# Two 7x7 involutions and a residual convolution block: the next strip's transposes issued between a stage's last tap product and its first column product

## The chip, the cores and the metric

The kernel runs on one core of a Trainium2 chip. Time is the device time of one execution in microseconds (us). Before the change it is 1824.14 us, the median of 8 executions between 1815.97 and 1828.26. The profile shown here is of one of these executions, which took 1827.25 us.

The core's engines work side by side, each through its own list of instructions in order: TensorE (PE: matrix products, whose weight loads have a row of their own, PEld), VectorE (DVE), ScalarE (ACT), GpSimd (POOL) and SyncE (SP, which here only issues transfers). POOL also issues transfers. PE writes its products to PSUM; the other engines copy them from there to SBUF.

## The reference

The input is x, 4 images of 256 channels by 56 x 56, in float32. Four layers follow one another, each as x = x + f(group norm of x) with 32 groups:

- layer 0, an involution: per pixel, a 64-long vector h is made from the 256 channels, and from h a 7 x 7 kernel for each of 16 groups of 16 channels; the output is the sum over the 49 taps of kernel times shifted input;
- layer 1, two 3 x 3 convolutions with batch norms and a residual;
- layer 2, an involution with batch norms and relus;
- layer 3, a spatial and channel gate built on Fourier sums.

```python
h = einsum('bchw,oc->bohw', x, reduce_w) + reduce_b
kern = einsum('bchw,oc->bohw', h, span_w) + span_b      # 7*7 taps x 16 groups
out = (kern * patches).sum(axis=3)                      # patches: the 49 shifted copies of x
```

The change is in the function that does both involutions, layers 0 and 2.

## The kernel before

An involution layer works through 8 stages, one for each image `b` and each half `cb` of its channels (128 channels, 8 groups), so there are 16 stages in the program: 8 in layer 0, in the first 525 us, and 8 in layer 2, from 1250 us on. The convolutions of layer 1 lie between them. `in_order` fixes every engine's instructions in the order in which the code emits them, so nothing is reordered by a scheduler.

A stage has two parts.

**Taps** (`tap_matrices`, line 560). 32 groups of 6 tap products turn h into the matrix `kt`, which holds for each window of 9 x 14 input pixels and each output pixel in it the weight of that input pixel. A group's products go to one PSUM buffer, and are copied to `kt` with the bias added: by ACT for every third group (line 582, six instructions; groups 0, 3, ... 30), by DVE for the others (line 589; group 31 is the last).

**Columns** (`apply`, line 601). The image is cut into 7 columns of 8 pixels, and each column into 19 windows of 3 rows. For a column, PE multiplies the transposed input windows `xw` by `kt` (line 613): first part A, 20 products, then part B, 36 products, each part in a PSUM buffer of its own. ACT takes the first slice of each part (line 626 in layer 0, 628 in layer 2), DVE adds the others (line 633), and the result is added into the image: in layer 0 by POOL (line 638), in layer 2 by DVE (line 640). The very first product of A needs tap groups 0 to 15 alone; the second needs groups up to 31.

**Strips and windows.** The input of a column is first normalised into a strip of 128 channels by 14 pixel columns (`next_strip`): in layer 0 by POOL (line 381), in layer 2 by ACT (line 379). There is one strip tile, so a new strip is written only after the old one has been transposed. `next_windows` then transposes the strip with 7 PE transposes (line 398) into a PSUM buffer, copies it to `xw` with ACT (line 399), and shifts two further copies of it within `xw` by four transfers (lines 405 and 407; SP issues them, but in layer 0 POOL issues the last). `xw` has three tiles, and the windows made in column k of a stage serve column k+3.

In a column the code emits: the products and additions of `apply`, then `next_windows` (transposes, copy, transfers), then `next_strip`, then sums and whatever else is laid into that place. So on PE a column's products are followed by the transposes of a strip that was written during the column before's end; on POOL in layer 0 the order is two additions (638), the transfer (407), the strip (381); on ACT in layer 2 it is the first slices of A and B (628), the copy (399), the strip (379).

**PSUM buffers.** `two_banks` hands out four buffers in turn to whoever asks. A new user waits until the user four requests earlier has been read. In the steady columns the turn is A, B, transposes, A, B, transposes, and so on.

Layer 2 also carries gate work of the image before: POOL loads pieces of it, computes (lines 780 to 787) and stores them, in the stages of images 1 to 3.

Of the kernel before, what the change touches and what calls it, by code (L numbers as in the profile page):

```python
# [16 lines left out]
P = 128  # L17
# [18 lines left out]
Q = QY * QX  # L36
# [3 lines left out]
NSB = 7  # L40
# [31 lines left out]
def net_kernel(  # L72
# [19 lines left out]
    nc = tc.nc  # L92
# [34 lines left out]
    ident_sb = const.tile([P, P], F32, name="ident_sb")  # L127
# [152 lines left out]
    def involution_layer(layer, xin, xout, red, span, sb, xs_of, ahead=None, pending=None):  # L280

        with ExitStack() as es:
# [5 lines left out]
            def two_banks():  # L288

                return banks.tile([P, 2, 512], F32, name="ps")  # L290
# [66 lines left out]
            strips, xws = [], []  # L357
# [25 lines left out]
            def window(ty):  # L383

                k, j = divmod(ty, TY)
                return (0, NSB, 2 * NSB - 1)[j] + k

            def next_windows():

                if len(xws) == len(columns):  # L390
                    return
                flat = strips[len(xws)].rearrange("p h w -> p (h w)")
                xw = work.tile([Q, NTY, P], F32, name="xw", bufs=NXW)
                xws.append(xw)

                ps = two_banks().rearrange("p i n -> p (i n)")
                for k in range(NSB):
                    nc.tensor.transpose(ps[:Q, k * P : (k + 1) * P], flat[:, k * Q : (k + 1) * Q], ident_sb)  # L398
                nc.scalar.copy(xw[:, :NSB, :], ps[:Q, : NSB * P].rearrange("q (n c) -> q n c", n=NSB))  # L399

                n = NSB - 1
                for j in range(1, TY):
                    cut = TY * QX * j
                    at = window(j)
                    nc.sync.dma_start(xw[: Q - cut, at : at + n, :], xw[cut:Q, 0:n, :])  # L405
                    eng = nc.sync if layer == 2 or j == 1 else nc.gpsimd
                    eng.dma_start(xw[Q - cut : Q, at : at + n, :], xw[:cut, 1 : 1 + n, :])
# [152 lines left out]
            def tap_matrices(b, cb, hooks):  # L560

                hp = h_of[b]
                kt = big.tile([Q, GB, TP // PB, NT, PB], F32, name="kt")
                for n in range(GB // 2 * TP // PB):
                    gp, pb = divmod(n, TP // PB)
                    ps = two_banks()
                    for k in range(PB):
                        py, px = divmod(pb * PB + k, TX)
                        z0 = ZF - py * QX - px
                        for i in range(2):  # L570
                            nc.tensor.matmul(  # L571
                                ps[:Q, i, k * NT : (k + 1) * NT],
                                z_sb[i * R : (i + 1) * R, cb * GB // 2 + gp, z0 : z0 + Q],
                                hp[i * R : (i + 1) * R, py, px].rearrange("p a t -> p (a t)"),
                                start=True,
                                stop=True,
                            )
                    g0, p0 = 2 * gp, pb * PB
                    if n % 3 == 0:
                        for i in range(2):  # L580
                            for k in range(PB):
                                nc.scalar.activation(  # L582
                                    kt[:, g0 + i, pb, :, k],
                                    ps[:Q, i, k * NT : (k + 1) * NT],
                                    AF.Identity,
                                    bias=zb_sb[:, cb * GB + g0 + i, p0 + k : p0 + k + 1],
                                )
                    else:
                        nc.vector.tensor_tensor(  # L589
                            kt[:, g0 : g0 + 2, pb],  # L590
                            ps[:Q, :, : PB * NT].rearrange("q i (k t) -> q i t k", k=PB),
                            zb_sb[:, cb * GB + g0 : cb * GB + g0 + 2, p0 : p0 + PB]
                            .unsqueeze(2)
                            .to_broadcast([Q, 2, NT, PB]),
                            ALU.add,
                        )
                    for h in hooks.get(n, ()):
                        h()
                return kt
# [348 lines left out]
            for i in range(NXW):  # L948
                hooks0.setdefault(2 + 5 * i, []).extend((next_windows, next_strip))
# [34 lines left out]
            for u, (b, cb) in enumerate(units):  # L984
# [21 lines left out]
                if b + 1 < B:  # L1006
                    n = 16 if layer == 0 else (26, 21)[cb]
# [8 lines left out]
                elif last_image:  # L1016
                    place(hooks, g2, (1,))
                    hooks.setdefault(16, []).append(ahead[0])
                kt = tap_matrices(b, cb, hooks)

                early = [[] for _ in range(NTX)]
                late = [[] for _ in range(NTX)]
# [46 lines left out]
                for tx in range(NTX):  # L1069
                    if layer == 2 and u == len(units) - 1 and tx == NTX - 1:  # L1070
                        column_sums(tx - 1)
                    for f in early[tx]:
                        f()
                    apply(b, cb, kt, tx, xws[u * NTX + tx])
                    next_windows()
                    next_strip()
                    if tx > 0 and not (layer == 2 and u == len(units) - 1 and tx == NTX - 1):
                        column_sums(tx - 1)
                    for f in late[tx]:
                        f()  # L1080
# [553 lines left out]

    ahead = [begin_conv] + [lambda part=part: begin_weights(part) for part in range(3)]
    st = involution_layer(0, src[0], src[1], red0, span0, sb0, {}, ahead)
    blocks = {}

# [4 lines left out]

    pending = conv_layer(src[1], src[2], st, begin_last)
    involution_layer(2, src[2], src[3], red2, span2, sb2, blocks, pending=pending)


# [63 lines left out]
```

## Time and profile before

| | us |
|---|---|
| median of 8 executions | 1824.14 |
| the profiled execution | 1827.25 |
| its span, from first to last instruction | 1825.1 |
| PE busy | 1725.1 |
| DVE busy | 1375.7 |
| ACT busy | 846.2 |
| POOL busy | 429.3 |
| PE busy in 0 to 525 us, layer 0 | 490.88 |
| PE busy in 525 to 1250 us, layer 1 | 715.04 |
| PE busy in 1250 to 1825 us, layer 2 and the gate | 519.15 |

Several views are used. The page's groups list, for each line and engine, the number of instructions, their busy time and the engine's idle time just before them, with what ended it. The timeline lists an engine's instructions in order of time, neighbours of one line merged: start, length, what, and in brackets the idle time before it and what ended that. The view of waits adds up such idle times. The chain of waits follows the work that ended last back from releaser to releaser.

### The profile page before, as it was taken

What the parts mean: (1) busy time and instruction counts of PE and PEld (TensorE: products, weight loads), DVE (VectorE), ACT (ScalarE), POOL (GpSimd) and SP (SyncE); (2) the same over time, 40 slices, a digit from 0 to 9 for tenths busy, and PEclk for the clock granted to TensorE, in tenths of its full rate; (3) what the DMA queues carried; (4) which work ended last, traced back from release to release, by engine and by line L of the source; (5) the groups of instructions that cost most, each with busy time, mean ns of one, the idle gap of its engine ahead of it and who ended that gap; (6) DMA issues with size and microseconds to landing.
All of it is one profiled execution on the core that took longest, in us unless ns stands there. A gap on an engine that the chain in (4) does not pass through costs nothing.

```text
span 1825.1 us, 55841 instructions
## 1 busy us (share of the span) xinstructions
PE 1725.1 (95%) x24034; PEld 1518.1 (83%) x24034; DVE 1375.7 (75%) x2729; ACT 846.2 (46%) x1981; POOL 429.3 (24%) x626
## 2 busy tenths in 40 slices
PE   7999999999899999999999999997999899899898
PEld 6898889888878988998899889985977787787786
DVE  3787777776689988898889988874777587677675
ACT  3666556555542312322222212104767567567564
POOL 2333432245210000000000000000000564563672
PEclk9999999999989999999999999998999899999996
DMA  2545534454641201111111111132534666765653
GB/s 85 157 151 165 164 116 147 152 157 131 196 161 54 69 26 62 63 69 38 62 60 59 59 42 33 38 129 68 165 129 132 180 207 182 207 207 157 188 151 109
DMA packets 66003, 215.75 MB, mean 118 GB/s; under 512 B 13237, under 2 KB 20926, under 8 KB 62046
## 3 DMA queue, kind: packets, MB, share of 16 engines
q1 hardware_dynamic: 48718, 145.24, 25.3%
q0 software_dynamic: 14688, 64.78, 11.1%
q8 instruction: 189, 3.10, 0.7%
q10 hardware_dynamic: 2352, 2.18, 0.4%
q14 instruction: 56, 0.46, 0.1%
HBM read 76.30 MB, written 49.15 MB: 69 GB/s over the span
## 4 chain that ended last, share of the span: by engine, by line
PE 77%; DVE 8%; ACT 6%; DMA 5%; issue 2%; SPq 1%; POOL 0%; ACTq 0%; DVEq 0%; POOLq 0%
PE mm L1482 19%; PE ps L571 17%; PE ps L613 16%; PE mm L1400 10%; PE mm L1371 5%; PE ps L398 4%; DMA xw<-xw 4%; ACT kt L582 4%; PE ps L450 1%; DVE kt L589 1%; ACT xw L399 1%; DVE un L633 1%; PE ps L696 1%; ACT hp L469 1%; SPq L405 1%
## 5 line engine op out<-in xcount | busy, mean ns | idle before, releaser
L613 PE MATMUL ps<-kt,xw 126*32 126x48 f32 (+1 forms) x12544 | 383.5, 236 | 41.6 <-DMA xw<-xw 15.2
L613 PEld LDWEIGHTS ps<-kt,xw 126*32 126x32 f32 (+1 forms) x12544 | 344.4, 123 | 86.9 <-issue 46.1
L571 PE MATMUL ps<-hp,z_sb 64*126 64x133 f32 x6144 | 391.9, 281 | 15.2 <-ACT kt L582 7.5
L571 PEld LDWEIGHTS ps<-hp,z_sb 64*126 64x126 f32 x6144 | 368.9, 187 | 33.4 <-ACT kt L582 13.5
L1482 PE MATMUL mm<-v,u_sb 128*128 128x280 f32 (+1 forms) x1728 | 385.0, 384 | 3.4 <-DVE v L1307 3.4
L589 DVE TENSOR_TENSOR kt<-ps,zb_sb 126x798 f32<-126x798 f32 x336 | 319.7, 981 | 89.3 <-PE ps L571 88.8
L1482 PEld LDWEIGHTS mm<-v,u_sb 128*128 128x128 f32 x1728 | 327.5, 190 | 57.9 <-DVE v L1307 3.8
L582 ACT ACTIVATE kt<-ps,zb_sb 126x133 f32<-126x133 f32 x1056 | 307.5, 443 | 94.2 <-PE ps L571 93.5
L1400 PE MATMUL mm<-v,u_sb 128*128 128x252 f32 (+1 forms) x936 | 212.0, 387 | 2.6 <-DVE v L1291 2.6
L1400 PEld LDWEIGHTS mm<-v,u_sb 128*128 128x128 f32 x936 | 177.7, 191 | 33.3 <-issue 2.7
L1519 POOL DMA_DIRECT2D x<-xs x24 | 13.1, 547 | 682.7 <-DVE xs L1518 427.4
L633 DVE SCALAR_TENSOR_TENSOR un<-ps,s,un 128x240 f32<-128x240 f32 x224 | 102.4, 457 | 94.4 <-ACT un L628 90.3
L633 DVE SCALAR_TENSOR_TENSOR un<-ps,par_sb,un 128x240 f32<-128x240 f32 x224 | 97.9, 456 | 91.0 <-ACT un L626 86.7
L1467 ACT ACTIVATE res<-xs,shift,norm_sb 128x1120 f32<-128x1120 f32 (+1 forms) x24 | 30.2, 1259 | 235.1 <-DVE xs L1518 107.2
L399 ACT COPY xw<-ps 126x896 f32<-126x896 f32 x112 | 101.7, 908 | 48.1 <-PE ps L398 39.5
L638 POOL TENSOR_TENSOR xs<-un,xs 128x240 f32<-128x240 f32 x112 | 72.3, 666 | 199.6 <-DVE un L633 199.6
L398 PE MATMUL ps<-ident_sb,strip_sb 128*126 128x128 f32 x784 | 111.0, 282 | 0.7 <-DVE un L633 0.7
L626 ACT ACTIVATE un<-ps,par_sb 128x240 f32<-128x240 f32 x112 | 50.3, 449 | 120.7 <-PE ps L613 119.4
L628 ACT ACTIVATE un<-ps,bn_t,s 128x240 f32<-128x240 f32 x112 | 60.2, 539 | 89.4 <-PE ps L613 85.0
L1371 PE MATMUL mm<-xs,u_sb 128*128 128x126 f32 (+1 forms) x792 | 98.5, 277 | 1.2 <-DVE xs L1334 0.9
L139 POOL TENSOR_TENSOR norm_sb<-norm_sb,mhalf 128x1 f32<-128x1 f32 x32 | 19.8, 620 | 334.5 <-DVE norm_sb L138 334.4
L1371 PEld LDWEIGHTS mm<-xs,u_sb 128*128 128x128 f32 x792 | 94.4, 191 | 2.4 <-issue 1.0
(254 smaller groups left out, 1996.5 us busy)
## 6 DMA issues: line engine op xcount, KB each, us to landing
xw<-xw SPq DMA_DIRECT2D x168, 252.0 KB
xw<-xw SPq DMA_DIRECT2D x224, 126.0 KB
xw<-xw POOLq DMA_DIRECT2D x56, 252.0 KB, 4.6
xs<-x SPq DMA_DIRECT2D x24, 560.0 KB
x<-xs POOLq DMA_DIRECT2D x8, 1568.0 KB, 8.4
xs<-x SPq DMA_DIRECT2D x8, 1568.0 KB
xs<-in_x_dram SPq DMA_DIRECT2D x6, 1568.0 KB
x<-xs SPq DMA_DIRECT2D x6, 1568.0 KB
```

Of the source, the lines that this page charges most:

```text
L398: nc.tensor.transpose(ps[:Q, k * P : (k + 1) * P], flat[:, k * Q : (k + 1) * Q], ident_sb)
L399: nc.scalar.copy(xw[:, :NSB, :], ps[:Q, : NSB * P].rearrange("q (n c) -> q n c", n=NSB))
L571: nc.tensor.matmul(ps[:Q, i, k * NT : (k + 1) * NT], z_sb[i * R : (i + 1) * R, cb * GB // 2 + gp, z0 : z0 + Q], hp[i * R : (i + 1) * R, py ...
L582: nc.scalar.activation(kt[:, g0 + i, pb, :, k], ps[:Q, i, k * NT : (k + 1) * NT], AF.Identity, bias=zb_sb[:, cb * GB + g0 + i, p0 + k : p0 ...
L589: nc.vector.tensor_tensor(kt[:, g0 : g0 + 2, pb], ps[:Q, :, : PB * NT].rearrange("q i (k t) -> q i t k", k=PB), zb_sb[:, cb * GB + g0 : cb ...
L613: nc.tensor.matmul(v[m * j : m * j + m, i, :, k * TP : (k + 1) * TP], xw[:, window(ty), m * j : m * j + m], kt[:, ng * j : ng * j + ng, :, ...
L628: nc.scalar.activation(part, o[0], AF.Identity, bias=bn["t4"][:, cb : cb + 1], scale=bn["s4"][ng][:, 0, cb : cb + 1])
L633: nc.vector.scalar_tensor_tensor(part, o[e], s, part, ALU.mult, ALU.add)
L638: nc.gpsimd.tensor_tensor(dst, u, dst, ALU.add)
L1371: nc.tensor.matmul(ps[:, co * m : (co + 1) * m], u[ci][:, co * P : (co + 1) * P], v2[:, e, : n // 2, ci * WT : (ci + 1) * WT], start=(ci = ...
L1400: nc.tensor.matmul(ps, u1_sb[:, ci, dy, k, co * P : (co + 1) * P], v[:, k, dy * NB + ci : (dy + n - 1) * NB + ci + 1 : NB, :], start=(j == 0),
L1482: nc.tensor.matmul(ps, u2_sb[:, ci, dy, k, co * P : (co + 1) * P], v[:, k, dy * NB + ci : (dy + n - 1) * NB + ci + 1 : NB, :], start=(j == 0),
```

## The change

The 7 transposes and the PSUM buffer that they write are taken out of `next_windows` into `begin_windows`. `next_windows` calls it only where it has not been called already, so columns 1 to 6 of every stage, and the windows made during the first stage's taps, are as before. At the end of each stage's `tap_matrices` the code now calls `begin_windows` once. With that, the transposes that stood behind the last product of column 0 stand ahead of its first one. The ACT copy, the transfers and the next strip stay where they were, behind the additions of column 0. The PSUM buffer is asked for before that of column 0's part A, so the turn of the buffers at the head of a stage is transposes, A, B, A, B, transposes, A, and so on.

```diff
+            begun_windows = []
+
+            def begin_windows():
+
+                flat = strips[len(xws)].rearrange("p h w -> p (h w)")
+                ps = two_banks().rearrange("p i n -> p (i n)")
+                begun_windows.append(ps)
+                for k in range(NSB):
+                    nc.tensor.transpose(ps[:Q, k * P : (k + 1) * P], flat[:, k * Q : (k + 1) * Q], ident_sb)
+
             def next_windows():
 
                 if len(xws) == len(columns):
                     return
-                flat = strips[len(xws)].rearrange("p h w -> p (h w)")
+                if not begun_windows:
+                    begin_windows()
+                ps = begun_windows.pop()
                 xw = work.tile([Q, NTY, P], F32, name="xw", bufs=NXW)
                 xws.append(xw)
 
-                ps = two_banks().rearrange("p i n -> p (i n)")
-                for k in range(NSB):
-                    nc.tensor.transpose(ps[:Q, k * P : (k + 1) * P], flat[:, k * Q : (k + 1) * Q], ident_sb)
                 nc.scalar.copy(xw[:, :NSB, :], ps[:Q, : NSB * P].rearrange("q (n c) -> q n c", n=NSB))
...
                 kt = tap_matrices(b, cb, hooks)
 
+                begin_windows()
+
                 early = [[] for _ in range(NTX)]
```

## The prediction

> **What bounds the kernel now.** The page first. PE is busy nearly throughout, and the chain of waits runs over it.
>
> ```profile
> PE 1725.1 (95%) x24034; PEld 1518.1 (83%) x24034; DVE 1375.7 (75%) x2729; ACT 846.2 (46%) x1981; POOL 429.3 (24%) x626
> ...
> PE 77%; DVE 8%; ACT 6%; DMA 5%; issue 2%; SPq 1%; POOL 0%; ACTq 0%; DVEq 0%; POOLq 0%
> ...
> L398 PE MATMUL ps<-ident_sb,strip_sb 128*126 128x128 f32 x784 | 111.0, 282 | 0.7 <-DVE un L633 0.7
> ```
>
> So only PE's idle time is to be won, and the transposes (line 398) hardly wait for anything today. The view of waits for PE says where products of line 613 do:
>
> ```profile
> PE ps L613 <- DMA xw<-xw: 15.2, 8, 3.4
> PE ps L613 <- ACT kt L582: 11.0, 13, 0.9
> PE ps L613 <- DVE sf L762: 2.5, 3, 0.9
> ```
>
> The last two lines are 16 waits of at most 0.9 us: one per stage. PE's timeline at the third stage of layer 0 shows the place.
>
> ```profile
> 170.63 14.18 PE L571 MATMUL ps<-hp,z_sb 64*126 64x133 f32 x240 [0.17 <-ACT kt L582]
> 184.73 0.41 PE L613 MATMUL ps<-kt,xw 126*64 126x96 f32 x2
> 185.98 3.22 PE L613 MATMUL ps<-kt,xw 126*64 126x96 f32 x110 [0.84 <-ACT kt L582]
> 189.13 0.98 PE L398 MATMUL ps<-ident_sb,strip_sb 128*126 128x128 f32 x7
> 190.05 3.24 PE L613 MATMUL ps<-kt,xw 126*64 126x96 f32 x112
> 193.22 0.98 PE L398 MATMUL ps<-ident_sb,strip_sb 128*126 128x128 f32 x7
> ```
>
> Call the first column product's start E (184.73). The next needs the last `kt`, which comes at E+1.25. In between PE idles 0.84 us. In all 16 stages that second start lies at 1.25 to 1.26.
>
> **What the change moves.** Seven transposes per stage, 189.13 to the next product at 190.05: 0.92 us (0.91 in the chain of waits). Moved to E, they end at E+0.91, and the one early product (two passes) takes 0.12 more: E+1.03, still short of E+1.25. Column 0 then runs as before and ends 0.91 us after where it would have carried transposes, so PE reaches column 1 0.91 us earlier: at most 16 x 0.91 = 14.6 us. Nothing is added, no instruction on DVE, ACT, POOL or SP changes its place.
>
> New waits on PSUM, each costed at nothing. The transposes take the buffer of tap group 28, which DVE has read by 183.77, before E; part A that of 29, read by 184.68. In three stages of layer 2 gate products sit between, and part A takes the buffer of group 30, read by ACT at 1426.62, 0.57 after its E of 1426.05 and before the transposes end. Only part B of column 1 is new: it takes the transposes' buffer, so it waits for the ACT copy, behind column 0's first slice of B. By ACT's rows that slice ends at 189.75 and the copy takes 0.91: 190.66. Column 1 would start at 189.14, and its part A takes 2.1 (from 190.05 to 192.33 when ACT takes it up, less 0.15): part B at 191.2. In layer 2 the same sum leaves 0.5 too. Were this cover gone, everything behind on PE would wait by the excess.
>
> Now what is late next: the transposes of column 1. They need the next strip. In layer 0 POOL makes it, by its timeline in the same stage:
>
> ```profile
> 190.28 1.29 POOL L638 TENSOR_TENSOR xs<-un,xs 128x240 f32<-128x240 f32 x2 [18.02 <-DVE un L633]
> 191.52 0.58 POOL L407 DMA_DIRECT2D xw<-xw  x1
> 192.15 1.00 POOL L381 TENSOR_SCALAR strip_sb<-xs,norm_sb 128x784 f32<-128x784 f32 x1
> ```
>
> POOL runs without a break from column 0's additions to the strip's end at 193.15, and its start hangs on DVE's slices of column 0, which stand at E+1.25 as before. The transposes start at 193.22 today, 0.07 later. PE would now be there at 192.31, and must wait until 193.2. The copy coming earlier (189.75 for 190.20) doesn't help: the transfer of line 407 waits for the additions (191.57), not for the copy (191.11). So in layer 0 the gain is given back one column on, with all of column 2 queued behind the waiting transposes. Strip end to transposes is, over the eight stages, 0.20, 0.07, 0.07, 0.10, 0.10, 0.12, 0.07 and 0.10 us. The handover itself takes between nothing and 0.07, the smallest seen, so layer 0 wins between 0.83 and 0.27 us together. I take 0.3, the handover having a price in every row.
>
> In layer 2 ACT makes the strip, and earlier:
>
> ```profile
> 1432.29 1.05 ACT L379 ACTIVATE strip_sb<-xs,norm_sb 128x784 f32<-128x784 f32 x1
> 1434.58 0.98 PE L398 MATMUL ps<-ident_sb,strip_sb 128*126 128x128 f32 x7
> ```
>
> Strip ready at 1433.34, transposes at 1434.58: 1.24 us to spare, and the copy ahead of it on ACT starts 0.36 earlier. So the 0.91 passes column 1 in all eight stages of layer 2: at most 7.3 us.
>
> There transfers decide. In the two stages before gate work starts no column waits for `xw`: 2 x 0.91 = 1.8. The six others (from 1426) keep the DMA engines 53 to 70% busy (the others of layer 2: 41%), and PE waits in four of them, worst here:
>
> ```profile
> 1447.80 2.51 PE L613 MATMUL ps<-kt,xw 126*64 126x96 f32 x28 [3.44 <-DMA xw<-xw]
> ```
>
> Column 3 needs its windows 0.91 earlier, but their copy, and so SP's four transfers, start only 0.36 to 0.45 earlier; for column 4 both move by 0.91. If the engines have room, a stage keeps its 0.91; if landing times hang on the gate's traffic, which POOL paces by itself, it keeps nothing. More than 0.91 or a loss needs the traffic to fall in another order: the same column waited 2.17 to 3.44 in its three worst stages, so 1.3 either way is the spread that order alone makes. I take the middle of nothing and 0.91, 0.45, as no row is nearer to one end: 6 x 0.45 = 2.7.
>
> Sum: 0.3 + 1.8 + 2.7 = 4.8 us. Against the profiled execution (span 1825.1, with 2.15 around it 1827.25) that is 1822.4; that execution is 3.1 above the median, so on the median 1824.14 - 4.8 = **1819.3**. Bounds of its terms: 0.3 + 1.8 + 0 = 2.1 and 0.8 + 1.8 + 5.5 = 8.1 saved, that is 1816.0 to 1822.0.
>
> **A rule on POOL and DVE.** In the changed kernel column 1's slices on DVE (line 633) lie 0.9 us earlier, over the strip on POOL (192.15 to 193.15) instead of over its last 0.3 us. The trace has a pair that suffers from such an overlap: line 640 on DVE, 0.41 us median, 1.38 at most, beside the gate work on POOL. The Trainium skill, SBUF — State Buffer, section "SBUF: two separate sides", says that the two share a port pair under an exclusive lock, which DVE takes with two SBUF inputs or in a two-port mode. Line 640 has two SBUF inputs, and agrees; line 633 reads one from PSUM, so by that rule the strip keeps its 1.00 us and the sum stays. If any overlap counted, layer 0 would lose instead (third rival). No row of before shows a strip wholly under line 633.
>
> **Rivals.**
> - *The strip is no limit.* POOL's spans are called rough by the page; if the strip is usable well before its recorded end, layer 0 keeps 8 x 0.91 = 7.3 and the whole is 16 x 0.91 = 14.6: 1809.5. For it: the transposes have never been seen to wait, so the true time of the strip is only bounded from above. Against: POOL's order is fixed, and the additions that precede the strip are real.
> - *Transfers take all.* The six loaded stages give back everything: 2.1 saved, 1822.0. For it: the waits of up to 3.44; against: POOL issues its second round of gate transfers at 1438.18, and with the change all four transfers of column 1's windows (1436.53 to 1439.04 today) would go out by then. The Trainium skill, DMA: Bandwidth & Descriptors, section "Issuing engines are not separate DMA queues", has SP's and POOL's transfers interleave on the same 16 engines. By that rule alone this case comes out; the latencies in the loaded stages agree.
> - *POOL's strip is slowed by DVE.* At 0.74 us a stage, what line 640 was once slowed by in the row at 1435.73 (1.15 for 0.41 us), layer 0 loses 8 x 0.74 = 5.9 in place of winning 0.3: 1825.5, no change.
> - *Slower: the shifted windows run into the gate's transfers.* Column 3 has its windows with little to spare in the loaded stages (one waits 0.50 already, at 1638.82), and loses half a microsecond of it; if a transfer falls behind a gate piece, a column waits like the 3.44 above. Two such new waits in each of three stages cost 6 x 2.5 = 15 less 4.8: 1834. It decides from 1.7 us lost per loaded stage (10.3 in all: 4.8 plus 5.5).
>
> **Chances.** 0.3% is 5.5 us, about what a measurement of this kernel can tell from no change: below 1818.7 is faster. Forecast 0.55; no limit by the strip 0.13; transfers take all 0.14; slowed strip 0.08; collisions 0.10. The forecast lies 0.6 us from the bound, so a little under half of it, 0.27, is faster: with the first rival 0.40. Same: 0.28 + 0.14 + 0.08 = 0.50. Slower: 0.10. The range takes in the forecast, the transfers' case, the slowed strip and the nearer part of the first rival: 1811 to 1826; the forecast's own is 1816 to 1822.
>
> **What would show it.** PE's timeline at E: 7 transposes, then the two early passes, then a wait of about 0.2 us in place of 0.84, the second product still at E+1.25. Layer 0: the transposes at the end of column 1 with an idle time of about 0.85 released by POOL's strip, column 2 starting where it did. Layer 2: no wait there, column 1 0.91 us earlier, and in the loaded stages waits for `xw` in columns 3 to 5 larger by about 0.45 a stage. The prediction is wrong if the layer 0 wait is missing, if part B of column 1 waits for the copy, or if the `xw` waits change by more than the gain.

## The result, and the profile after

| | before | after |
|---|---|---|
| median of the runs that were compared, us | 1824.58 (66 runs) | 1816.83 (24 runs) |
| ratio of times, 95% interval | | 0.996 [0.9949, 0.9971] |
| the profiled execution, us | 1827.25 | 1819.61 |
| its span, us | 1825.1 | 1817.8 |

The change saves 0.4%: (1 - 0.996) x 1824.58 = 7.3 us, by the interval 5.3 to 9.3. The forecast was 4.8 us saved and 1819.3 us.

In the changed kernel the transposes are line 396, the column products 622, the tap products 580, the copies to `kt` 591 (ACT) and 598 (DVE), the additions on DVE 642 and on POOL 647, the copy to `xw` 408 and POOL's transfer 416. The strips keep their lines, 381 on POOL and 379 on ACT. These are the page's rows for PE, for the chain of waits, and for the transposes (the last column: idle time just before them, and what ended it).

```profile
PE 1723.3 (95%) x24034; PEld 1515.5 (83%) x24034; DVE 1378.8 (76%) x2729; ACT 843.9 (46%) x1981; POOL 431.1 (24%) x626
...
PE 77%; DVE 8%; ACT 5%; DMA 4%; issue 2%; POOL 2%; SPq 1%; ACTq 0%; POOLq 0%; DVEq 0%
...
L396 PE MATMUL ps<-ident_sb,strip_sb 128*126 128x128 f32 x784 | 110.7, 282 | 5.8 <-POOL strip_sb L381 5.6
```

PE does the same work. POOL has gone from 0 to 2% of the chain, and the transposes, which hardly waited before (0.7 us), now wait 5.6 us for POOL's strip. The view of waits for PE (total, times, longest) says the same, and that the sixteen waits of column products for the last `kt` are gone: no line of 622 names ACT's `kt` or DVE's `sf` any more.

```profile
PE ps L622 <- issue: 15.7, 17, 2.0
PE ps L622 <- DMA xw<-xw: 13.7, 11, 4.9
...
PE ps L396 <- POOL strip_sb L381: 5.6, 8, 0.8
```

The place itself, the third stage of layer 0, on the timelines of PE, POOL and DVE (start, length, what, and in brackets the idle time before it):

```profile
183.48 0.98 PE L396 MATMUL ps<-ident_sb,strip_sb 128*126 128x128 f32 x7
184.39 6.77 PE L622 MATMUL ps<-kt,xw 126*64 126x96 f32 x224
191.94 0.98 PE L396 MATMUL ps<-ident_sb,strip_sb 128*126 128x128 f32 x7 [0.78 <-POOL strip_sb L381]
```

```profile
189.02 1.30 POOL L647 TENSOR_TENSOR xs<-un,xs 128x240 f32<-128x240 f32 x2 [18.02 <-DVE un L642]
190.26 0.58 POOL L416 DMA_DIRECT2D xw<-xw  x1
190.89 1.00 POOL L381 TENSOR_SCALAR strip_sb<-xs,norm_sb 128x784 f32<-128x784 f32 x1
```

```profile
190.70 1.81 DVE L642 SCALAR_TENSOR_TENSOR un<-ps,par_sb,un 128x240 f32<-128x240 f32 x4 [0.88 <-ACT un L635]
```

E is, as in the prediction, the place right behind the last tap product, where the first column product stood before: 184.73 there, 183.47 here. Two columns, 224 products, now follow the transposes with no idle time that this view counts; between the starts of the second early pass and the second product 0.19 us are left, where 1.10 lay before. Then PE stands 0.78 us until the strip that ends at 191.89 (190.89 + 1.00). From E to that strip's end it is 8.42 us, as it was before the change (from 184.73 to 193.15). The length of a stage is taken here and below from the start of its last tap product (0.20 us ahead of E) to the start of its last column product: 29.18 us against 29.19, so nothing is kept.

In layer 2 ACT makes the strip. The same place in its second stage, on PE and on ACT:

```profile
1348.18 0.98 PE L396 MATMUL ps<-ident_sb,strip_sb 128*126 128x128 f32 x7
1349.09 6.76 PE L622 MATMUL ps<-kt,xw 126*64 126x96 f32 x224
1355.78 0.98 PE L396 MATMUL ps<-ident_sb,strip_sb 128*126 128x128 f32 x7
```

```profile
1353.14 0.90 ACT L408 COPY xw<-ps 126x896 f32<-126x896 f32 x1
1353.92 1.05 ACT L379 ACTIVATE strip_sb<-xs,norm_sb 128x784 f32<-128x784 f32 x1
```

The strip ends at 1354.97 (1353.92 + 1.05), 0.81 us ahead of the transposes that read it, and they follow the products without a gap. This stage went from 35.44 to 34.57 us.

With the gate's traffic beside it a stage can still lose all of it. Here, in the stage whose last tap product starts at 1419.82, PE gets as far as the first 8 products of column 4 (counted from 0), and waits for windows:

```profile
1436.67 0.62 PE L622 MATMUL ps<-kt,xw 126*64 126x96 f32 x8
1442.21 4.43 PE L622 MATMUL ps<-kt,xw 126*64 126x96 f32 x104 [4.92 <-DMA xw<-xw]
```

In the same column of the same stage the wait was 3.44 us before, and the stage is 0.3 us longer than it was (35.42 for 35.12).

Two other loaded stages, the second halves of images 1 and 2 in layer 2, lose part of it at the first product of column 2. These are PE, DVE and POOL in the first of the two:

```profile
1493.86 3.26 PE L622 MATMUL ps<-kt,xw 126*64 126x96 f32 x112 [0.65 <-ACT xw L408]
```

```profile
1489.81 0.87 DVE L649 SCALAR_TENSOR_TENSOR xs<-un,xs 128x240 f32<-128x240 f32 x1
...
1491.06 0.88 DVE L649 SCALAR_TENSOR_TENSOR xs<-un,xs 128x208 f32<-128x208 f32 x1
...
1492.25 1.46 DVE L642 SCALAR_TENSOR_TENSOR un<-ps,s,un 128x240 f32<-128x240 f32 x3
```

```profile
1489.26 1.15 POOL L795 TENSOR_TENSOR gn<-gn,sfb 128x448 f32<-128x448 f32 x1
1490.49 1.21 POOL L796 TENSOR_TENSOR gx<-gx,gn 128x448 f32<-128x448 f32 x1
```

Products of line 437, for the next image, stand between the transposes and column 2 there and take a PSUM buffer in the turn, so column 2's part A gets the buffer of column 1's part A. DVE has read it at 1493.71 (1492.25 + 1.46), and the product starts 0.15 us later; in the second of the two stages it starts 0.14 us after DVE's read, and there the profile names DVE. DVE is late because two of its additions of line 649 lie beside POOL's sums for the gate and take 0.87 and 0.88 us. In the changed kernel without gate work (below) the same two take 0.41 and 0.37, and PE doesn't wait. In all six profiled executions that have the move in layer 2 and the whole gate work, both stages have this wait, 0.18 to 0.91 us each; in no execution without the move does either have it.

Stage lengths, added up from PE's timeline, in the two profiled executions:

| us | before | after |
|---|---|---|
| layer 0, stages 1 to 7 | 231.8 | 232.9 |
| layer 0, stage 8 | 34.3 | 30.6 |
| layer 2, the two stages without gate work | 64.77 | 62.99 |
| layer 2, the six with it | 212.4 | 210.9 |

These two executions differ by 7.3 us in span, the same as the change saves by the ratio, but that they agree is chance: half of it, 3.8 us, is stage 8 of layer 0, through waits for windows (4.1 us before, 1.0 after) that scatter from one execution to the next. Other executions with the move in layer 0 and the late strip have 30.8 to 32.8 us for this stage, and others without it 31.3 to 33.3.

### The profile page after: what moved, and what is told of

Its sections match the earlier page's. It is cut to its first block, busy times and chain, and to the rows that moved or that the text cites. A ratio compares the mean times of both kernels' runs of the same rounds, so it can differ in the third digit from the quotient of the medians.

```text
span 1817.8 us, 55835 instructions
## 1 busy us (share of the span) xinstructions
PE 1723.3 (95%) x24034; PEld 1515.5 (83%) x24034; DVE 1378.8 (76%) x2729; ACT 843.9 (46%) x1981; POOL 431.1 (24%) x626
## 4 chain that ended last, share of the span: by engine, by line
PE 77%; DVE 8%; ACT 5%; DMA 4%; issue 2%; POOL 2%; SPq 1%; ACTq 0%; POOLq 0%; DVEq 0%
PE mm L1493 20%; PE ps L580 17%; PE ps L622 14%; PE mm L1411 10%; PE mm L1382 5%; PE ps L396 5%; DMA xw<-xw 4%; ACT kt L591 2%; PE ps L459 2%; DVE un L642 1%; DVE kt L598 1%; ACT xw L408 1%; SPq L414 1%; PE ps L705 1%; PE ps L928 1%
## 5 line engine op out<-in xcount | busy, mean ns | idle before, releaser
L622 PE MATMUL ps<-kt,xw 126*32 126x48 f32 (+1 forms) x12544 | 379.3, 236 | 32.6 <-issue 15.7
L396 PEld LDWEIGHTS ps<-ident_sb,strip_sb 128*126 128x126 f32 x784 | 84.2, 141 | 16.7 <-POOL strip_sb L381 6.8
```

The source lines that it names most:

```text
L622: nc.tensor.matmul(v[m * j : m * j + m, i, :, k * TP : (k + 1) * TP], xw[:, window(ty), m * j : m * j + m], kt[:, ng * j : ng * j + ng, :, ...
```

## The experiments

**The change in one layer at a time.** First the changed kernel once more, beside the two halves of it, to have all three on one chip against the same runs of before.

> The changed kernel itself once more, beside the three kernels that take it apart, for the same chip and a second profile. Both theories: 7 to 8 us (0.996) faster than before, as recorded. If the 2.9 us beyond the forecast 4.8 come from chance in one profile (the last stage of layer 0 is 3.8 us shorter in it), the second profile shows that stage at another length; if the change brings them, at the same.

Measured: 1818.66 us against 1823.36, ratio 0.9965 [0.9949, 0.9981], 6.4 us saved (3.5 to 9.3). The last stage of layer 0 took 31.6 us in this execution against 30.6 in the first profile, and 32.1 in the kernel that moves nothing in layer 0 (below): most of its 3.8 us was chance.

```diff
-                begin_windows()
+                if layer == 0:
+                    begin_windows()
```

> Transposes ahead of column 0 in layer 0 alone. Theory of the strip: each of the 8 stages gives its 0.91 us back at column 1's transposes, 0.3 us in all stays (0 to 0.8): ratio 1.000. Rival, both layers gain alike: half of what the change brings, 3.9 us, 0.998. Rival, the gain beyond the forecast sits at the end of layer 0: about 3 us, 0.998. The profile tells the two apart: eight waits of 0.7 to 0.85 us for POOL's strip at the end of column 1 under the first theory.

Measured: 1824.71 us, ratio 1.0001 [0.9986, 1.0016]. The waits of PE in it:

```profile
PE ps L396 <- POOL strip_sb L381: 6.1, 8, 0.8
```

Eight waits, one per stage of layer 0, of 0.76 us on average, in place of eight of 0.85: what is won at the first product is paid at the strip. That the strip is no limit, that both layers gain alike, or that some 3 us of the gain sit at the end of layer 0, is out by this ratio.

```diff
-                begin_windows()
+                if layer == 2:
+                    begin_windows()
```

> Transposes ahead of column 0 in layer 2 alone. Theory of the strip: all that the change brings, 7 to 7.5 us (7.3 is eight times 0.91), 0.996, with no wait for a strip. Rival, both layers gain alike: 3.9 us, 0.998. Rival, the gain beyond the forecast sits at the end of layer 0: 4.5 us, 0.9975.

Measured: 1819.33 us, ratio 0.998 [0.9964, 0.9996], 3.6 us saved (0.7 to 6.6). In layer 0 (the window from 60 to 500 us) the old waits are back and there is none for the strip:

```profile
PE ps L622 <- ACT kt L591: 6.8, 8, 0.9
```

So the gain is layer 2's, but it is half of the 7 to 7.5 us that were expected of it, which lie outside the interval. The halves add up to 3.4 us, below the 6.4 of both together, but their intervals are 3 us wide to each side, and the two don't contradict each other.

**The strip brought forward.** If the strip is what holds layer 0 back, an earlier strip must give the time back. The transposes have read the strip tile by E+0.91 now, so POOL, idle during the taps, can write the next one at once:

```diff
                 begin_windows()
+                if layer == 0:
+                    next_strip()
...
-                    next_strip()
+                    if layer == 2 or tx > 0:
+                        next_strip()
```

> The changed kernel, with column 0's next strip of layer 0 issued on POOL right behind the early transposes instead of behind column 0's additions (the strip tile is free by then, and POOL idles). Theory of the strip: the eight waits of column 1 for POOL (5.6 us in the profile after) go, and 8 x 0.85 = 6.8 us more stay: 14.5 us faster than before, 0.992, unless column 2's transposes wait next, for which POOL's chain of column 1 also starts 0.9 us earlier. Rival, the strip is only the label of the wait and another of its semaphores (DVE) ends it: as the changed kernel, 0.996.

Measured: 1815.26 us, ratio 0.9952 [0.9936, 0.9968], 8.8 us saved against before. And in a second series of the same kernel:

> The early strip once more, beside the two strips on the same chip. Theory, as its first run: even stages of layer 0 keep 0.85 us, odd ones 0.2 to 0.6, some 4.5 us in all on top of the change: 11 to 12 us less than before, 0.9938; its first run gave 0.9952 (0.9936 to 0.9968). Rival, the strip's relief is lost elsewhere: 7 us, 0.996, as the change alone.

Measured: 1811.92 us against 1825.83, ratio 0.9932 [0.9909, 0.9954], 12.4 us saved. It is the fastest kernel of this study that does all the work. Its waits from 60 to 500 us, and the third stage on PE and on POOL:

```profile
PE ps L396 <- POOL strip_sb L381: 0.8, 2, 0.4
```

```profile
183.43 0.98 PE L396 MATMUL ps<-ident_sb,strip_sb 128*126 128x128 f32 x7
184.34 6.78 PE L622 MATMUL ps<-kt,xw 126*64 126x96 f32 x224
191.05 0.98 PE L396 MATMUL ps<-ident_sb,strip_sb 128*126 128x128 f32 x7
```

```profile
184.60 0.99 POOL L381 TENSOR_SCALAR strip_sb<-xs,norm_sb 128x784 f32<-128x784 f32 x1 [13.62 <-PE ps L396]
```

The strip is ready at 185.59, the transposes come straight behind the products, and the stage takes 28.34 us instead of 29.18: it keeps 0.84 (in the second series 28.80 us, 0.38 kept). Stages 1 to 7 of layer 0 take 227.1 us (225.7 in the second series), against 230.8 to 232.9 in the five executions with moved transposes and the late strip, and 231.6 to 233.2 in the four without the move there. That shows the cause of layer 0's lost gain. The whole time tells the two kernels apart less well: 0.9952 here against 0.9965 for the changed kernel in the same series, with intervals that overlap.

The whole came out smaller than expected, though, and the second half of an image shows why. These are PE, DVE and POOL in the second stage (the first three second halves, which the expectations count as odd stages, keep 0.2 to 0.6 us here rather than 0.85):

```profile
134.34 0.98 PE L396 MATMUL ps<-ident_sb,strip_sb 128*126 128x128 f32 x7 [0.40 <-POOL strip_sb L381]
```

```profile
127.84 2.19 DVE L349 BATCH_NORM_STATS2 st<-xs 128x6 f32<-128x448 f32 x4
129.95 1.80 DVE L642 SCALAR_TENSOR_TENSOR un<-ps,par_sb,un 128x240 f32<-128x240 f32 x4
```

```profile
131.50 1.28 POOL L647 TENSOR_TENSOR xs<-un,xs 128x240 f32<-128x240 f32 x2 [1.96 <-DVE un L642]
132.73 0.52 POOL L416 DMA_DIRECT2D xw<-xw  x1
133.29 1.00 POOL L381 TENSOR_SCALAR strip_sb<-xs,norm_sb 128x784 f32<-128x784 f32 x1
```

One column further on the same chain binds again: four statistics instructions keep DVE 2.19 us, its additions follow at 129.95, POOL's wait for them, and the next strip, behind them on POOL, ends at 134.29 with the transposes at 134.34. This wait of 0.4 us stands in two of the four second halves, and in three in the second series; 0.27 us more follow each time at column 3, for DVE's additions.

**Two strip tiles.** Would layer 0 keep everything if the transposes never waited for POOL? In layer 0 two tiles take turns, and the next strip is put ahead of the column's additions.

```diff
+            strip_of = [strip_sb]
+            if layer == 0:
+                strip_of.append(wpool.tile([P, HS, QX], F32, name="strip2_sb"))
...
-                st = strip_sb
+                st = strip_of[len(strips) % len(strip_of)]
...
+                    if layer == 0:
+                        next_strip()
...
-                    next_strip()
+                    if layer == 2:
+                        next_strip()
```

> The changed kernel with two strip tiles in layer 0, so that POOL writes the next strip ahead of a column's additions, in every column. In the early strip's run the odd stages of layer 0 still wait at column 2, for a strip that comes behind additions held up by DVE's sums. Theory of the strip: no wait of the transposes in layer 0 at all, all eight stages keep 0.9 us, 13 to 14 us less than before (0.9925), 2 us less than with the early strip. Rival, the odd stages are held by DVE itself: as the early strip, 0.995.

Measured: 1816.31 us, ratio 0.9947 [0.9931, 0.9963], 9.7 us saved: not better than with the early strip. The waits from 60 to 520 us (line 626 is the column products here, 411 the copy to `xw`):

```profile
PE ps L626 <- issue: 6.3, 10, 1.5
PE ps L626 <- ACT xw L411: 2.8, 3, 0.9
PE ps L626 <- DMA xw<-xw: 2.7, 2, 1.4
```

No line has transposes waiting for a strip. The quiet third stage takes 28.31 us and keeps its 0.88, but stages 1 to 7 take 231.8 in this execution: other waits stand in the place, for the copy on ACT, for transfers, and 6.3 us that the profile calls issue (time in which PE waited for nothing that it shows). The three waits for ACT, 0.92 us each, are at column 3's first product in the first three second halves, where the early strip left at most 0.27, for DVE; the product starts 0.05 us after the copy of column 2's transposes ends, and why it needs that copy is not shown. The recorded rival, that DVE itself holds these stages, has the right ratio; what holds them is, by the profile, ACT's copy. So removing POOL from the chain does not by itself give the 7.3 us of eight stages.

**The gate work left out.** What the six loaded stages of layer 2 would keep is the term that the forecast could only bound. Without gate work in them there is nothing to collide with. Both kernels, before and changed, were run without the gate of images 0 to 2:

```diff
-                        chunks.extend(gate_chunk(b - 1, j, c) for j in range(NCHUNK) for c in range(NB))
```

> The kernel before without the gate work of images 0 to 2 in layer 2's stages (its loads, sums and stores are left out, so three of four images are not written). It is the base for the next run. Theory that the gate's transfers cause the waits for the windows: the waits of PE for xw in layer 2 (11.1 us in the profile before) go nearly to nothing, and the time falls by 10 to 20 us. Rival, the windows' own transfers are too slow: they stay above 6 us.

> The changed kernel with the same gate work left out; compared with the run before it, not with the full kernel. Theory that the gate's transfers take back part of the gain: without them all eight stages of layer 2 keep 0.91 us, 7.3 us and 0.3 of layer 0, so 7.6 us less than the run before (0.9958 of it), and every stage of layer 2 is 0.9 us shorter in its timeline. Rival, the loss in the loaded stages has another cause (PE's instructions arriving late, the windows' own transfers): 4 to 5 us, as in the full kernel, and some stages keep less than 0.5.

Measured: 1796.99 us, ratio 0.9844 [0.9825, 0.9863], for the kernel before; 1787.37 us, ratio 0.9797 [0.9776, 0.9818], for the changed one. By the ratios the change is worth 0.47%, 8.6 us, and by the medians 9.6. PE's waits in layer 2 (from 1280 to 1760 us), the kernel before without gates:

```profile
PE ps L613 <- ACT kt L582: 4.2, 5, 0.9
PE ps L613 <- DVE sf L762: 2.6, 3, 0.9
...
PE ps L613 <- issue: 1.0, 2, 0.8
...
PE ps L613 <- DMA xw<-xw: 0.3, 1, 0.3
```

and the changed one without gates:

```profile
PE ps L622 <- issue: 1.7, 3, 0.7
...
PE ps L622 <- DMA xw<-xw: 0.3, 1, 0.3
```

The first two lines, 6.8 us in eight waits, are gone and nothing has come for them. The six stages that were loaded take 182.1 us instead of 188.2: they keep 6.1 us, 1.0 a stage, slightly more than the 0.91 that was moved; all eight stages of layer 2 keep 7.2 us, 0.9 a stage. So where there is no gate work, the whole gain passes through layer 2.

The kernel before loses 28.5 us with its gates, by the ratio, more than the 10 to 20 that were expected. The six stages account for 24.2 of it (212.4 to 188.2), and the waits for windows and those called issue together for 16.4 (the view below against 0.3 and 1.7 us in the same stretch); the rest was not taken apart.

For comparison, the kernel before with its gates, from 1280 to 1792 us:

```profile
PE ps L613 <- DMA xw<-xw: 11.1, 6, 3.4
PE ps L613 <- issue: 7.3, 8, 2.2
```

**The gate's transfers without its sums.** Is it the gate's transfers or its work on POOL that makes the windows late? Both kernels with the four POOL instructions of the gate's sums left out, its loads and stores kept:

```diff
-                xn = work.tile([P, CR * W], F32, name="gn", bufs=1)
-                nc.gpsimd.tensor_scalar(xn, xs, rstd[...], shift[...], ALU.mult, ALU.add)
-                scale, bias = (t[:, cb : cb + 1] for t in gate_of[b])
-                nc.gpsimd.tensor_scalar(xs, xs, scale, bias, ALU.mult, ALU.add)
-                nc.gpsimd.tensor_tensor(xn, xn, sf, ALU.mult)
-                nc.gpsimd.tensor_tensor(xs, xs, xn, ALU.add)
```

> The kernel before with the gate's sums on POOL left out and its transfers kept (images 0 to 2 are stored without their gate). Theory that the transfers alone make the waits for the windows: PE's waits for xw in layer 2 stay at 8 to 15 us and the time within 10 us of before. Rival, POOL's sums slow DVE and this makes the stages long: the waits fall below 4 us and the time comes near the kernel without gate work, some 1797.

> The changed kernel with the same sums left out, compared with the run before it. Theory that the transfers take back the gain of the loaded stages: 2 to 5 us less than that run, and the six loaded stages of layer 2 together keep under half of 5.5 us. Rival, they keep it once POOL's sums are gone: 7.6 us, as without any gate work.

Measured: 1827.82 us, ratio 1.0007 [0.9985, 1.003], for the kernel before, and 1820.34 us, ratio 0.9984 [0.9963, 1.0005], for the changed one. The waits of the former from 1280 to 1792 us:

```profile
PE ps L613 <- DMA xw<-xw: 11.4, 9, 4.4
PE ps L613 <- issue: 9.7, 9, 2.7
```

They are those of the kernel before (11.1 and 7.3) and not those without gates (0.3 and 1.7 in this stretch). The transfers make the windows late; POOL's sums have no part in that which can be measured. What the sums do lengthen is DVE's additions of line 640: of 84 in the loaded stages 26 take over 0.6 us in the kernel before, and none over 0.41 without the sums. This is what the waits at column 2 above come from. The changed kernel of this pair can't confirm it, as other waits (1.11 and 0.60 us, called issue) make PE late at the same place. How much of the gain the traffic takes, this pair doesn't settle: the ratios differ by 4.2 us, the medians by 7.5, and the loaded stages of the two profiled executions by 8.7 (217.0 to 208.3). That is more than the move can give, and shows how far one execution scatters.

## Why the prediction came out as it did

**The place and the ceiling: as predicted.** The transposes stand at E, the two early passes behind them at E+0.91 and E+1.06, and the second product at E+1.25; in three stages of layer 2 what follows comes 0.07 to 0.09 us earlier, since a wait for `sf` is gone. Without gates the move was worth 0.9 us a stage over the eight of layer 2, the 0.91 of the transposes. No part B of column 1 waits for the ACT copy, which ends 0.7 us earlier: the PSUM waits that the prediction lists were rightly costed at nothing. It missed one, for the buffer of column 2's part A in two loaded stages: 0.65 and 0.57 us in the profile after.

**Layer 0: as predicted, and shown from both sides.** The expected wait was 0.85 us released by POOL's strip; it is 0.78 on the timeline and 5.6 us in eight. Kept by column 1's transposes, stage by stage against E: 0.15, 0.01, 0.02, 0.07, 0.08, 0.06, 0 and 0, together 0.4 us, where 0.3 was taken. The change in layer 0 alone has the ratio 1.0001, and an early strip removes the wait and gives the stage 0.84 us. The rival "the strip is no limit" falls with that: POOL's recorded ends hold to within the smallest handover seen.

**POOL's strip beside DVE: the rival falls.** In the changed kernel DVE's four slices (190.70 to 192.51) lie over the whole strip (190.89 to 191.89), and it takes 1.00 us, as it did before. The Trainium skill, SBUF — State Buffer, section "SBUF: two separate sides", has, of DVE's instructions, only those with two SBUF inputs or in a two-port mode take the exclusive lock that POOL's also take; line 642 reads one input from PSUM, and the trace agrees with it at 1.00 us.

**Layer 2 without load: as predicted.** The two stages went from 64.77 to 62.99, 1.8 us, the forecast's term; 64.85 in the kernel with layer 0's half alone and 62.95 with layer 2's half alone. Single executions scatter here too, from 62.9 to 63.8 with the move and the whole gate work.

**Layer 2 under load: the term that stays open.** The forecast took 2.7 us, the middle of nothing and 5.5, since no row was nearer to one end. If the other terms are as found, 7.3 - 0.4 - 1.8 = 5.1 would be left for the six stages. But the half in layer 2 alone gives 3.6 - 1.8 = 1.8 for them, and the stage lengths don't decide: unmoved 212.4 and 209.6 us, moved 210.9, 209.2, 214.8, 204.4, 207.9 and 212.6, means 211.0 and 210.0, with single executions 5 us off.

What is shown is the frame, 6.1 us where there are no gates and single stages that give everything back, as the one with the wait of 4.92 us, and one piece in between: the waits for DVE at column 2, 0.5 to 1.2 us together in the six executions, which the forecast had not seen. The forecast that the waits for `xw` grow by 0.45 a stage can't be read either: 11.1 and 10.2 us in total (1280 to 1792 us) in the two executions without the move in layer 2, 5.6 to 12.7 in the six with it. Nor were those waits the only term that scatters: PE's waits called issue, which the forecast left out, are as large, and the two kinds together come to 18.4 and 16.7 us without the move and to 16.9 to 24.6 with it.

The rival "transfers take all" (2.1 us saved) lies below the interval of 5.3 to 9.3 and so is out as a whole. The Trainium skill, DMA: Bandwidth & Descriptors, section "Issuing engines are not separate DMA queues", has transfers issued by POOL and SP interleave on the same 16 engines; the trace agrees, as leaving out all gate work takes the waits from 11.1 to 0.3 us and leaving out POOL's sums leaves them at 11.4.

**Slower by collisions: no.** The interval excludes it. One stage has the longer wait that this rival named (3.44 to 4.92 us, and 0.3 us lost), far from the 1.7 a stage at which it would decide.

**The sum.** 4.8 us was forecast between 2.1 and 8.1, 7.3 was measured (5.3 to 9.3), and 6.4 (3.5 to 9.3) in the second series: inside the bounds, with a point that lies below the interval of the first series and within that of the second. The time, 1816.8 us, lies in the forecast's own range of 1816 to 1822. That the sum came this near is partly luck: its largest term was the middle between two bounds and not a reading. At 0.4% it fell on the far side of the 0.3% bound, for which the chances had been put at 0.40 against 0.50 for no change: the forecast lay 0.6 us from that bound, and the one unsettled term was larger than that. If a term was mis-sized, it is the 2.7 us of the loaded stages, the only one that could hold 2.5 us more; that it was has not been shown.

**The experiments' own misses.** The early strip was expected to give 14.5 us and gave 8.8 in its first series (12.4 in the second, where 11 to 12 were expected); DVE's statistics, which hold the next strip in two or three of the four second halves, are the part of this that the traces show. Two tiles were expected to give 13 to 14 us, more than the early strip, and gave 9.7. The change in layer 2 alone was expected to give 7 to 7.5 us and gave 3.6; leaving out the gate work was expected to give 10 to 20 us and gave 28.5. With the gate's transfers alone the six loaded stages were expected to keep under half of 5.5 us, and the two profiled executions differ by 8.7, which is scatter.

## What to carry to other kernels

A bubble filled on the busiest engine is worth what the next producer's slack allows: read the end of what PE needs next against the time at which PE would now ask for it. Here 0.07 us of slack on POOL took back all but a few hundredths of 0.91 us, 1.24 us on ACT let it pass, and moving that producer too was what paid. Where shared transfers decide, a kernel with the traffic left out gives the ceiling (6.1 us in six stages here), but the part that is kept under load needs many timed runs: the scatter of one traced execution, 5 us, was as large as the whole term. And work that comes earlier meets the next thing that is late: here a PSUM buffer that DVE gives back late, because POOL works beside it.

## What was not expected of the hardware

PE's waits called "issue" are not spread at random. The changed kernel's PE timeline at the end of a loaded stage:

```profile
1707.00 2.55 PE L622 MATMUL ps<-kt,xw 126*64 126x96 f32 x50
1711.53 1.01 PE L622 MATMUL ps<-kt,xw 126*32 126x48 f32 x62 [1.98 <-issue]
...
1713.39 2.57 PE L622 MATMUL ps<-kt,xw 126*64 126x96 f32 x57
1717.85 0.93 PE L622 MATMUL ps<-kt,xw 126*32 126x48 f32 x55 [1.89 <-issue]
...
1719.62 2.64 PE L622 MATMUL ps<-kt,xw 126*64 126x96 f32 x64
1723.79 0.82 PE L622 MATMUL ps<-kt,xw 126*32 126x48 f32 x48 [1.53 <-issue]
```

The wait comes behind 50, 57 and 64 products of a column: 7 later each time, so every 126 matrix instructions (a column's 112 products and 7 transposes, and 7 more). Each has a weight load, which makes 252 instructions, and the page counts 189 packets in the larger of its two queues that bring instructions, 3.10 MB, 16.4 KB each. The Trainium skill, Perfetto Trace Analysis, section "The 4-stage abstract model", gives an instruction 64 bytes; 252 of them would be an estimated 16.1 KB, close to one packet. The waits grow with traffic: from 1280 to 1792 us they are 7.3 us in the kernel before, 9.7 with the gate's transfers alone and 1.7 without gate work, though they scatter (9.2 and 13.5 in two executions of the changed kernel). That PE's own instructions arrive late behind other transfers fits all of this, but no run here isolated it. If it is so, it is a price of transfers that no wait for a buffer shows.
